# A fused attention and feed-forward block on one core: the second batch's q is biased and squared ahead of the turning of x, and some scaling and transfers change engines

## The chip, the cores and the metric

The kernel runs on one core of a Trainium2 chip. A core has five engines with a queue of instructions each, worked off in order: TensorE (PE in the profile; PEld is its loading of weights), VectorE (DVE), ScalarE (ACT), GpSimd (POOL) and SyncE (SP). In this kernel SyncE and ScalarE also issue the transfers (DMA). The engines wait for one another by semaphores only. The metric is the time of one execution on the device, in microseconds.

## The reference

All arrays are float32. `x` has 8 batches of 1024 tokens of 256 channels.

```python
xn  = layernorm(x)                       # over the 256 channels, eps 1e-5
q, k, v = split(xn @ qkv_w + qkv_b)      # 16 heads of 16
q, k = q / |q|, k / |k|                  # per token and head
kv  = einsum('bhnd,bhne->bhde', k, v)    # no softmax: a 16 x 16 matrix per head
att = einsum('bhnd,bhde->bhne', q, kv) reshaped to (8, 1024, 256) @ proj_w + proj_b
ffn = relu(xn @ W1 + b1) @ W2 + b2       # 256 -> 1024 -> 256
out = x + att + ffn
```

## The kernel before

**Stages and rounds.** The program is one stream of work over the batches, written out by hand in the order in which each engine is to do it; no planner reorders it. For batch b there are two large stages. `hidden(b)` makes relu(xn W1 + b1) (`first_hidden` for batch 0), and `second(b)` multiplies it by W2 and adds the attention, the residual and the bias. Between them stands the projection of the next batch, `project_by_sums(b + 1)`, to q and k. So TensorE's order is: hidden(b), projection of b+1, second(b), hidden(b+1), and so on. Below, *round b* is the time from the first matmul of `second(b)` to the first of `second(b + 1)`.

**Fewer matmuls, more additions.** The products are formed with schemes that need fewer block products (7 for 8, and in `hidden` 26 for 32), at the price of sums of blocks before and after. GpSimd forms most sums of operands: `make_forms` (L319) those of the turned x, named s1A, dA, X1 to X10 and so on; `g_sums` (L693) those for the product of x and k; `sums_of_a` (L239 to L244) those of the hidden values and q. VectorE forms the sums of results out of the banks of PSUM, in `hidden` at L1004, in `second` at L1134 and L1151, and in the product of x and k at L734 (`u_g`, `gT`). In `hidden` several sums read a bank in the midst of its accumulation, so the next product into it waits for that sum; a new product also waits for a free bank among seven.

**From x to the turned x.** For batch b+2, `stats_of` computes mean and variance of the 1024 tokens on VectorE (L344 to L359; the square root on ScalarE, L349). `norm_apply` (L368 on ScalarE, L372 on VectorE) scales the 8 tiles of 128 tokens in place. `turn_x` then transposes 32 by 32 blocks on VectorE (L386, four instructions, one for each fourth j) and moves the blocks between partitions with four transfers for each j, 16 in all (L394), into `xnT`. `shift` (L656, ScalarE) afterwards adds one to half of x's channels in place, which folds a bias into the product of x and k.

**From q to the turned q.** In `second(b)` for batch b+1: `bias_in_bank` (L605) copies a difference of biases into PSUM, `bias_of_q` (L599) adds it to two of four parts of q on VectorE. `norms_of_q` squares the four parts on ScalarE (L504), sums over each head on VectorE (L505), takes maximum, root and reciprocal (`invert`, L465 to L467), and scales q on GpSimd (L624). In `hidden(b + 1)` q is turned as x is (`turn_q`, L386 and L394), at steps set by a table.

**second(b)** runs the products `a`, `c_`, `f`, `d`, the product of x and k (`mix_g_by_sums`: gpa, gpe, gpc, gpd, then gpa and gpd again, L728) and `e`; gpe has its last part between the two halves of `e`. `join` and `turn_back` add a result to `u`, transpose it on VectorE (`yt`, L1142) and add it to the residual on GpSimd (`xq`, L1147); `store` (L1110, SyncE) writes a half of the batch out. The hooks `early`, `mid`, `behind`, `late` and `later` place the work for the following batches; they differ for b of 0, 1 and above:

- b = 0: statistics of batch 2 in `early`, scaling of it in `mid`, `turn_next` (turning of x of batch 2) in `late` with the bias of q of batch 1 behind it; `norms_of_q(1)` in `later`.
- b = 1: bias and norms of q of batch 2 in `early`; statistics of batch 3 and its eight scalings on ScalarE in `mid`; `turn_next` in `behind`.
- b > 1: bias, norms and turning in `early`; statistics of x of batch b+3 in `later`; its scaling after `hidden` of the following round.

**Weights.** In `hidden`, the 26 combinations of W1 lie in DRAM (`w1f`) and are fetched two products at a time into five slots, by `load_w1` (L898) on SyncE. In SyncE's queue in round 0 stand in order: the transfers of the turned x, the load of x of batch 3 (L149), the store of one half, the weights 5 and 6, the store of the other half (which waits for GpSimd's last `xq`), the weights 7, 8 and 9, and the transfers of the turned q.

In `turn_next`, transfer r of each j goes to queue r modulo the number of queues given; before, batch 2 uses SyncE and ScalarE by turns, later batches SyncE alone.

Of the kernel before, what the change touches and what calls it, by code (L numbers as in the profile page):

```python
# [9 lines left out]
F32 = mybir.dt.float32  # L10
# [51 lines left out]
def kernel(  # L62
# [34 lines left out]
    nc = tc.nc  # L97
    P = 128
    B, N, C = x.shape
    H, D = 16, 16  # L100
    assert H * D == C
    INTER = w1.shape[1]
    NT = N // P
    HT = NT // 2
# [13 lines left out]
    one = ctx.enter_context(tc.tile_pool(name="one", bufs=1))  # L118
    work = ctx.enter_context(tc.tile_pool(name="work", bufs=2))
    small = ctx.enter_context(tc.tile_pool(name="small", bufs=2))  # L120
# [15 lines left out]
    def bank(shape, name):  # L136

        return psum.tile(shape, F32, tag="bank", name=name)
# [107 lines left out]
    HM, FH, HC = INTER // 2, FC // 2, C // 2  # L246
# [80 lines left out]
    def more_sums_of_x(b, part):  # L327

        names = [f"X{i}" for i in range(3 + 4 * part, 7 + 4 * part)]
        make_forms(forms_of(b) | more_forms_of(b), names)  # L330
# [29 lines left out]
            for t in tiles:  # L360
                stats[b, t] += (nmr,)

    def norm_apply(b, tiles):
        for t in tiles:
            xt, xn = xs[b][:, t, :], xns[b][:, t, :]
            i, mv, rstd, *nmr = stats.pop((b, t))
            if nmr:
                nc.scalar.activation(  # L368
                    xn, xt, AF.Identity, bias=nmr[0][:, i : i + 1], scale=rstd[:, i : i + 1]
                )  # L370
            else:
                nc.vector.tensor_scalar(  # L372
                    xn, xt, mv[:, i, 0:1], rstd[:, i : i + 1], ALU.subtract, ALU.mult
                )

    class Turn:
# [21 lines left out]
        def step(self, queues=(nc.sync,)):  # L398
            self.square()
            self.move(queues)  # L400
# [3 lines left out]
    def turn_x(b, queues=(nc.sync,)):  # L404

        if b not in xnTs:
            xnTs[b] = big.tile([P, KC, NP, P, 2], F32, tag="xnT", name=f"xnT_{b}")
            turns["x", b] = Turn(xnTs[b], xns[b], f"x_{b}")
        turns["x", b].step(queues)
# [53 lines left out]
    def invert(ss):  # L463

        nc.vector.tensor_scalar_max(ss, ss, L2_EPS * L2_EPS)  # L465
        nc.scalar.activation(ss, ss, AF.Sqrt)
        nc.vector.reciprocal(ss, ss)  # L467
# [30 lines left out]

        return qks[b][:, m, 2 * u : 2 * u + 2, :]

    def squares_of(b, u, m, ss, tag="yt"):
        pool = work if tag == "yt" else one
        sq = pool.tile([P, 2, C], F32, tag=tag, name=f"sq_{b}_{u}_{m}")
        nc.scalar.activation(sq, part_of_qk(b, u, m), AF.Square)  # L504
        return lambda: nc.vector.tensor_reduce(  # L505
            ss[:, 2 * u : 2 * u + 2, :],
            sq.rearrange("p w (g d) -> p w g d", d=D), AX.X, ALU.add,
        )
# [82 lines left out]
            norms_of[b, h, 1] = ss[:, ts(h, HT), :]  # L591
            scale(nc.gpsimd, b, h, 1)

    def bias_of_q(b, bias=None):
        if bias is None:
            bias = bias_in_bank(b)
        for u in (3, 0):
            q1 = part_of_qk(b, u, 0)
            nc.vector.tensor_tensor(  # L599
                q1, q1, bias.unsqueeze(1).to_broadcast([P, 2, C]), ALU.add  # L600
            )

    def bias_in_bank(b):
        bias = bank([P, C], f"dbias_{b}")
        nc.scalar.copy(bias, dbias)  # L605
        return bias

    def norms_of_q(b):
        ss = small.tile([P, NT, H], F32, tag="ssq", name=f"ssq_{b}", bufs=1)
        late = []  # L610
        for u in range(NP):
            late.append(squares_of(b, u, 0, ss, ("u1", "y")[u % 2] if b == 1 else "yt"))
            if len(late) == 2:
                late.pop(0)()
        late.pop(0)()
        invert(ss)
        for h in range(2):
            norms_of[b, h, 0] = ss[:, ts(h, HT), :]
            scale(nc.gpsimd, b, h, 0)
# [492 lines left out]
    def second(b, early=None, mid=None, behind=None, late=None, later=None):  # L1112
# [36 lines left out]
        def join(n, m, bank_, u):  # L1149
            y = tmp("y")  # L1150
            nc.vector.scalar_tensor_tensor(y, bank_, ob[:, 2, m : m + 1], u, ALU.add, ALU.add)  # L1151
            turn_back(n, m, y)
# [112 lines left out]
        u1 = tmp("u1")  # L1265
# [21 lines left out]
        product(e, t1, s1, True, False)  # L1287
        join(1, 1, e, u3)
        next(of_g)
        more_sums_of_x(b + 1, 1)  # L1290
        later()
        store(b, 1)
        product(e, b22, s4, False, True)
        join(0, 1, e, u2)


    warm = bank([P, HT, P], "warm")
# [82 lines left out]
    for b in range(B):  # L1380
# [26 lines left out]
        else:  # L1407
# [3 lines left out]
                norm_apply(b + 2, range(NT))  # L1411
            project_by_sums(b + 1)

        def turn_next():
            if b + 2 < B:
                for _ in range(R):
                    turn_x(b + 2, (nc.sync, nc.scalar) if b == 0 else (nc.sync,))
                shift(b + 2)

        def early():  # L1420
# [14 lines left out]
        def mid():  # L1435
            if b == 0:
                norm_apply(2, range(NT))
                next(of_w1)
                load_first_w1()
            elif b == 1:  # L1440
                stats_of(3)
                norm_apply(3, range(NT))

        def behind():
            if b == 1:
# [1 line left out]

        def late():
            if b == 0:
                bias = bias_in_bank(1)  # L1450
                turn_next()
                bias_of_q(1, bias)
            if b + 3 < B:
                load(b + 3)

        def later():
            if b == 0:
                norms_of_q(1)
            else:
                stats_of(b + 3)  # L1460

# [32 lines left out]
```

## Time and profile before

| | us |
|---|---|
| median of 3 runs (604.47 to 604.97) | 604.96 |
| the profiled execution, its own time | 604.75 |
| its span, first to last instruction | 603.0 |
| round 0 (67.18 to 141.79) | 74.61 |
| round 1 (141.79 to 216.36) | 74.57 |
| round 2 (216.36 to 289.22) | 72.86 |
| round 3 (289.22 to 362.09) | 72.87 |

The profile is one execution. Its instructions are listed by engine, with start and duration counted from the first instruction, the line of the kernel, the operation, the tiles written and read, their shapes, and in brackets the idle time of the engine before the instruction and what ended it. Equal neighbours are merged, with their number behind an x. Matmuls are pipelined and a row's start and end are modelled, so a hole in TensorE's work is best read by laying rows of one round against those of another. `PEclk` is the clock that TensorE was granted, as a share of full speed. In a table by stretches, each engine has its busy time and the number of its instructions; at the end stand the granted clock, the mean busy share of the 16 DMA engines, and GB/s.

### The profile page before, as it was taken

What the parts mean: (1) busy time and instruction counts of PE and PEld (TensorE: products, weight loads), DVE (VectorE), ACT (ScalarE), POOL (GpSimd) and SP (SyncE); (2) the same over time, 40 slices, a digit from 0 to 9 for tenths busy, and PEclk for the clock granted to TensorE, in tenths of its full rate; (3) what the DMA queues carried; (4) which work ended last, traced back from release to release, by engine and by line L of the source; (5) the groups of instructions that cost most, each with busy time, mean ns of one, the idle gap of its engine ahead of it and who ended that gap; (6) DMA issues with size and microseconds to landing.
All of it is one profiled execution on the core that took longest, in us unless ns stands there. A gap on an engine that the chain in (4) does not pass through costs nothing.

```text
span 603.0 us, 7997 instructions
## 1 busy us (share of the span) xinstructions
PE 596.5 (99%) x2385; PEld 413.2 (69%) x2385; DVE 435.4 (72%) x803; ACT 247.4 (41%) x525; POOL 481.0 (80%) x453
## 2 busy tenths in 40 slices
PE   9999999999999999999999999999999999999997
PEld 5466656786568865688566894678846787468746
DVE  7987976878758785577856878388873669537773
ACT  4654332473405851158311673126730373203810
POOL 2859999988976889769897698976989679983470
PEclk9999999999999999999999999999999999999999
DMA  8545367784056733377134780356702667006704
GB/s 289 87 101 140 82 211 206 183 210 55 10 158 170 194 48 70 108 202 179 19 71 139 197 172 6 99 137 178 158 22 49 144 144 148 2 0 164 185 11 95
DMA packets 164810, 73.02 MB, mean 121 GB/s; under 512 B 147488, under 2 KB 152736, under 8 KB 163872
## 3 DMA queue, kind: packets, MB, share of 16 engines
q1 hardware_dynamic: 154432, 67.31, 46.6%
q10 hardware_dynamic: 10336, 5.21, 3.1%
q8 instruction: 19, 0.31, 0.2%
q14 instruction: 23, 0.19, 0.1%
HBM read 44.44 MB, written 11.80 MB: 93 GB/s over the span
## 4 chain that ended last, share of the span: by engine, by line
PE 86%; DVE 6%; POOL 3%; DMA 2%; ACT 1%; issue 1%; ACTq 0%; DVEq 0%; POOLq 0%
PE ph L985 23%; PE poe L1103 9%; PE poa L1103 9%; PE pod L1103 5%; PE poc L1103 5%; PE pof L1103 4%; PE pqe L530 3%; PE pqa L530 3%; PE pqd L530 3%; PE gpd L728 2%; PE gpe L728 2%; PE gpa L728 2%; PE pqc L530 2%; POOL qk L624 2%; PE tok L1213 2%; PE pq L428 1%
## 5 line engine op out<-in xcount | busy, mean ns | idle before, releaser
L1012 ACT ACTIVATE hT<-hT,b_sb 128x256 f32<-128x256 f32 x224 | 95.7, 497 | 56.1 <-DVE hT L1004 56.1
L1004 DVE TENSOR_TENSOR hT<-ph,hT 128x512 f32<-128x512 f32 x84 | 56.0, 687 | 25.1 <-ACT hT L999 21.6
L1004 DVE TENSOR_TENSOR hT<-hT,ph 128x512 f32<-128x512 f32 x77 | 51.8, 679 | 11.1 <-PE ph L985 7.0
L1103 PE MATMUL poa<-hT,w_sb 128*128 128x512 f32 x120 | 56.2, 593 | 0.0
L504 ACT ACTIVATE sq<-qk 128x512 f32<-128x512 f32 x56 | 34.2, 627 | 49.9 <-DVE qk L536 39.8
L1147 POOL TENSOR_TENSOR xq<-xq,yt_o 128x512 f32<-128x512 f32 x29 | 36.5, 1272 | 22.1 <-DVE yt_o L1142 22.1
L985 PE MATMUL ph<-xnT,w_sb 128*128 128x256 f32 x224 | 52.9, 379 | 0.0
L985 PE MATMUL ph<-qk,w_sb 128*128 128x256 f32 x196 | 48.1, 379 | 0.3 <-DMA w_sb<-w1f 0.3
L239 POOL TENSOR_TENSOR hS<-hT 128x512 f32<-128x512 f32 x30 | 38.3, 1276 | 11.5 <-DVE hT L1004 11.5
L985 PEld LDWEIGHTS ph<-xnT,w_sb 128*128 128x128 f32 x224 | 41.9, 190 | 5.5
L985 PEld LDWEIGHTS ph<-qk,w_sb 128*128 128x128 f32 x196 | 37.2, 190 | 5.7 <-POOL Mt L234 0.7
L999 ACT COPY hT<-ph 128x512 f32<-128x512 f32 x49 | 28.1, 574 | 30.4 <-PE ph L985 30.3
L240 POOL TENSOR_TENSOR hS<-hS,hT 128x512 f32<-128x512 f32 x30 | 38.3, 1277 | 2.4
L1103 PEld LDWEIGHTS poa<-hT,w_sb 128*128 128x128 f32 x120 | 22.7, 190 | 25.4 <-issue 22.7
L242 POOL TENSOR_TENSOR hT<-hT 128x512 f32<-128x512 f32 x30 | 38.5, 1310 | 0.0
L1142 DVE STREAM_TRANSPOSE yt_o<-y_o 128x512 f32<-128x512 f32 x29 | 32.2, 1112 | 8.3 <-ACT y_o L1272 6.1
L244 POOL TENSOR_TENSOR hS<-hT,hS 128x512 f32<-128x512 f32 x30 | 37.7, 1290 | 0.0
L985 PE MATMUL ph<-xS,w_sb 128*128 128x256 f32 x140 | 35.1, 381 | 0.2
L624 POOL TENSOR_TENSOR qk<-qk,ssk 128x1024 f32<-128x1024 f32 x14 | 26.8, 1936 | 9.3 <-DVE ssk L467 9.3
L1151 DVE SCALAR_TENSOR_TENSOR y_o<-poe,ob,u_o 128x512 f32<-128x512 f32 x14 | 10.4, 741 | 31.1 <-PE poe L1103 31.1
L1103 PE MATMUL poe<-hS,w_sb 128*128 128x512 f32 x64 | 30.4, 600 | 0.3
L1103 PE MATMUL poc<-hS,w2t 128*128 128x512 f32 x64 | 29.9, 592 | 0.0
(249 smaller groups left out, 1422.4 us busy)
## 6 DMA issues: line engine op xcount, KB each, us to landing
w_sb<-w1f SPq DMA_DIRECT2D x49, 256.0 KB, 3.5
qT<-turn_q SPq DMA_DIRECT2D x128, 64.0 KB, 3.0
x<-in_L_attn_x_dram SPq DMA_DIRECT2D x15, 512.0 KB, 4.6
xq<-in_L_attn_x_dram SPq DMA_DIRECT2D x60, 128.0 KB, 5.0
out_dram<-xq SPq DMA_DIRECT2D x58, 128.0 KB, 2.9
w_sb<-w1f SPq DMA_DIRECT2D x7, 1024.0 KB, 4.9
xnT<-turn_x SPq DMA_DIRECT2D x104, 64.0 KB, 2.1
w1t<-w1f SPq DMA_DIRECT2D x14, 256.0 KB, 5.3
```

Source lines behind the costliest of these rows:

```text
L239: eng.tensor_tensor(s1, a21, a22, ALU.add)
L240: eng.tensor_tensor(s2, s1, a11, ALU.subtract)
L242: eng.tensor_tensor(a21, a11, a21, ALU.subtract)
L244: eng.tensor_tensor(s4, a12, s2, ALU.subtract)
L530: nc.tensor.matmul(dst[:, w, :], f[pairs[g][2][i]][:, :, w], pairs[g][3][i], start=start and w == 0, stop=stop, skip_group_check=True,)
L624: eng.tensor_tensor(part, part, norms_of[b, h, s].unsqueeze(3).to_broadcast([P, HT, H, D]), ALU.mult,)
L728: nc.tensor.matmul(dst, l[:, t, :], r[:, t, :], start=start and t == 0, stop=stop and t == HT - 1, skip_group_check=True,)
L985: nc.tensor.matmul(banks[chain][:, t], w[:, t, :], f[v], start=start and t == 0, stop=n == last[chain], skip_group_check=True,)
L1004: nc.vector.tensor_tensor(block(v), operand(p), operand(q), ALU.add if op == "+" else ALU.subtract)
L1012: nc.scalar.activation(part, part, AF.Relu, bias=b1_sb[:, fc : fc + 1])
L1103: nc.tensor.matmul(dst, l, r, start=start and n == 0, stop=stop and n == len(lhs) - 1, skip_group_check=True,)
L1147: nc.gpsimd.tensor_tensor(xh, xh, yt.rearrange("p u w r c -> p (u w) r c"), ALU.add)
```

## The change

Five edits, all for batches 0 and 1:

1. In `second(0)`, the bias of q of batch 1 and the four squarings come first, and the turning of x of batch 2 after them. The squares no longer use the scratch tiles `u1` and `y`, but four blocks of `hS` (plane 2). The sums over heads, the root and the scaling stay in `later`.
2. In `second(0)`, the last four sums of x of batch 1 (X7 to X10, GpSimd) come at the end, behind the last `join`, and no longer ahead of `later`. On GpSimd they thus stand behind the scaling of q and the last `xq`.
3. In `second(1)`, four of the eight scalings of x of batch 3 are done by VectorE (tiles 0 to 3, L372's form), and ScalarE does tiles 4 to 7 first. On VectorE the four stand between `nmr` and the `yt` of the first result.
4. Of the 16 transfers of the turned x of batch 2, ScalarE issues 4 where it issued 8; SyncE issues 12.
5. Of the 16 of batch 3, ScalarE issues 4 where it issued none; SyncE issues 12.

The number of instructions on every engine stays the same but for the four scalings and the transfers; TensorE's order is unchanged.

```diff
-    def norm_apply(b, tiles):
+    def norm_apply(b, tiles, on_vector=False):
...
-            if nmr:
+            if nmr and not on_vector:
...
-    def squares_of(b, u, m, ss, tag="yt"):
-        pool = work if tag == "yt" else one
-        sq = pool.tile([P, 2, C], F32, tag=tag, name=f"sq_{b}_{u}_{m}")
+    def squares_of(b, u, m, ss, sq=None):
+        if sq is None:
+            sq = work.tile([P, 2, C], F32, tag="yt", name=f"sq_{b}_{u}_{m}")
...
+    def norms_of_second_q():
+
+        ss = small.tile([P, NT, H], F32, tag="ssq", name="ssq_1", bufs=1)
+        late = [
+            squares_of(
+                1, u, 0, ss,
+                hSs[0][:, 2, i].rearrange("p u c w -> p (u c w)").rearrange("p (w c) -> p w c", w=2),
+            )
+            for u, i in enumerate((0, 2, 3, FH))
+        ]
+        yield
+        for step in late:
+            step()
+        invert_and_scale_q(1, ss)
+        yield
+
+    def invert_and_scale_q(b, ss):
         invert(ss)
         for h in range(2):
             norms_of[b, h, 0] = ss[:, ts(h, HT), :]
...
         next(of_g)
-        more_sums_of_x(b + 1, 1)
+        if b > 0:
+            more_sums_of_x(b + 1, 1)
         later()
         store(b, 1)
         product(e, b22, s4, False, True)
         join(0, 1, e, u2)
+        if b == 0:
+            more_sums_of_x(b + 1, 1)
...
+        of_q = []
+
         def turn_next():
             if b + 2 < B:
                 for _ in range(R):
-                    turn_x(b + 2, (nc.sync, nc.scalar) if b == 0 else (nc.sync,))
+                    turn_x(b + 2, (nc.sync,) * 3 + (nc.scalar if b < 2 else nc.sync,))
                 shift(b + 2)
...
             elif b == 1:
                 stats_of(3)
-                norm_apply(3, range(NT))
+                norm_apply(3, range(HT, NT))
+                norm_apply(3, range(HT), True)
...
         def late():
             if b == 0:
-                bias = bias_in_bank(1)
+                bias_of_q(1)
+                of_q.append(norms_of_second_q())
+                next(of_q[0])
                 turn_next()
-                bias_of_q(1, bias)
...
         def later():
             if b == 0:
-                norms_of_q(1)
+                next(of_q[0])
```

## The prediction

> **What bounds the kernel now.** I read the page's busy times first, then the table by rounds, the matmuls in order of time where a round is long, and VectorE, GpSimd and SyncE at those places.
>
> ```profile
> PE 596.5 (99%) x2385; PEld 413.2 (69%) x2385; DVE 435.4 (72%) x803; ACT 247.4 (41%) x525; POOL 481.0 (80%) x453
> ```
> TensorE is the bound, so only its holes can be won. A round is taken from the first `poa` of one batch to that of the next:
> ```profile
> 67.18:141.79 74.61, 73.79 (x300) 51.62 (x299) 59.50 (x117) 33.88 (x75) 70.86 (x65) 1.00 0.73 181
> 141.79:216.36 74.57, 73.56 (x300) 51.94 (x299) 56.22 (x114) 35.04 (x76) 62.07 (x59) 1.00 0.49 117
> 216.36:289.22 72.86, 72.81 (x299) 52.03 (x298) 52.62 (x97) 30.95 (x67) 61.74 (x59) 1.00 0.50 120
> 289.22:362.09 72.87, 72.82 (x299) 52.03 (x298) 52.60 (x97) 30.96 (x67) 61.70 (x59) 1.00 0.49 120
> ```
> The first number is the length. Rounds 0 and 1, which alone the change touches, are 1.75 and 1.71 us over round 2: 3.4 us (0.57%) is all there is to win. TensorE's rows laid against round 2 show where:
> ```profile
> 111.57 1.03 PE L985 MATMUL ph<-xnT,w1t 128*128 128x256 f32 x4
> 112.98 1.10 PE L985 MATMUL ph<-xnT,w1t 128*128 128x256 f32 x4 [0.38 <-DVE hT L1004]
> ...
> 119.25 1.97 PE L985 MATMUL ph<-qk,w_sb 128*128 128x256 f32 x8 [0.30 <-DMA w_sb<-w1f]
> ...
> 168.47 1.13 PE L728 MATMUL gpd<-gt,x 128*128 128x128 f32 x8 [0.60 <-DVE u_g L734]
> ...
> 188.29 1.10 PE L985 MATMUL ph<-xnT,w1t 128*128 128x256 f32 x4 [0.27 <-DVE hT L1004]
> ```
> Round 0 loses 0.54 at 112.98, 0.53 more by 117.82, 0.65 at 119.25: 1.72. Round 1 loses 0.85 at 168.47 and 0.86 from 188.29 to 191.32. VectorE, then GpSimd, around them:
> ```profile
> 106.05 0.95 DVE L467 RECIPROCAL ssq<-ssq 128x128 f32<-128x128 f32 x1 [0.38 <-ACT ssq L466]
> ...
> 110.95 1.31 DVE L386 STREAM_TRANSPOSE turn_q<-qk 128x512 f32<-128x512 f32 x2 [0.59 <-POOL qk L624]
> ...
> 158.13 0.44 DVE L359 SCALAR_TENSOR_TENSOR nmr<-mv,rstd 128x8 f32<-128x8 f32 x1
> 158.50 1.12 DVE L1142 STREAM_TRANSPOSE yt_o<-y_o 128x512 f32<-128x512 f32 x1
> 162.68 2.49 DVE L386 STREAM_TRANSPOSE turn_x<-x 128x512 f32<-128x512 f32 x4 [3.07 <-ACT x L368]
> ...
> 177.68 1.41 DVE L344 BATCH_NORM_STATS2 st<-x 128x6 f32<-128x256 f32 x4 [1.61 <-DMA x<-in_L_attn_x_dram]
> ```
> ```profile
> 107.08 3.83 POOL L624 TENSOR_TENSOR qk<-qk,ssq 128x1024 f32<-128x1024 f32 x2 [0.81 <-DVE ssq L467]
> ...
> 158.50 4.98 POOL L244 TENSOR_TENSOR hS<-hT,hS 128x512 f32<-128x512 f32 x4
> ```
> The reader sees two chains. In round 0 the norms of q come late, GpSimd's scaling of q ends at 110.9, and VectorE's queue stands behind `turn_q`. In round 1 VectorE waits 3.07 us for ScalarE's eight scalings and passes the delay on to `u_g`; later it waits for the load of x, queued on SyncE behind 16 transfers.
>
> **Part 1, round 0: bias and squares lead, last sums later, 12 transfers on SyncE.** On VectorE the two biases (1.25) and four turnings (2.48) change places; both end at 98.1 as before. ScalarE squares from 95.7, when the second bias is done: 4 at 0.63, to 98.1 (before: from 102.10). Their scratch in `hS` was last read by `gpe` and `gpc`, over at 91.5. ScalarE then issues 4 transfers instead of 8 (eight took 5.85, so 2.9) and reaches `shift` at 101.0, as before. VectorE's four reductions start at 100.6, behind `gT`, instead of 102.75, and need 2.5 unhindered. The maximum (0.23) waits for GpSimd to end `xq` (103.4), root 0.31, reciprocal 0.95: 104.8 against 107.0. GpSimd, relieved of X7 to X10 (2.9), scales from 104.9 to 108.7, against 110.9. `turn_q` then never waits, and the add that frees TensorE at 112.98 runs near 111, before it is wanted at 112.43.
>
> What is pushed back: X7 to X10 run at 110.0 to 112.9; the first is wanted at 121.9. GpSimd's sums of x follow 0.7 later and meet two VectorE adds with two SBUF inputs (one such row took 1.08 instead of 0.64 at 114.89); I charge 0.1. SyncE issues 12 transfers, not 8, at 0.66: to 104.4, not 100.6. Behind them the load of x, one store and two loads of weights end at 109.9 instead of 107.75; landing 3.4 later, at 112.1 and 113.3, they precede their matmuls (114.2, 115.9). The turned x lands by 109 (4.5, the slowest but one) and is first read at 114.70; the x loaded 3 us later is read at 154.29. The second store waits for GpSimd's `xq`, now done at 110.0 instead of 112.15; so the third weights are issued at 112.7, not 114.89, and with the 4.22 that they took land at 116.9, before 117.6. Gain: 1.72 - 0.1 = 1.6.
>
> **Part 2, round 1: VectorE scales 4 tiles; 4 of 16 transfers on ScalarE.** ScalarE ends four scalings at 160.6 instead of 162.65 (0.49 apart). VectorE's four stand between `nmr` (158.57) and `yt`, while GpSimd runs without a gap. What one costs depends on that:
> ```profile
> L372 DVE TENSOR_SCALAR x<-x,mv,rstd x7: 404/413/1476, 6.3 to 11.8; 128x256 f32<-128x256 f32 x7
> ```
> ```profile
> 11.85 1.27 POOL L234 TENSOR_TENSOR w1t<-w_sb 128x512 f32<-128x512 f32 x1 [10.55 <-DMA w_sb<-in_L_ffn_W_dram]
> 13.20 1.28 POOL L234 TENSOR_TENSOR w1t<-w_sb,w1t 128x512 f32<-128x512 f32 x1
> ```
> The one of 1476 ns is the only one under a GpSimd add: it began at 11.79 and ended at 13.27, 0.15 after that add. Six without one took 0.41 (0.33 apart). A run of them under a busy GpSimd is not shown; the nearest, two-input adds of both engines in the last stage, go strictly by turns:
> ```profile
> 572.57 1.64 DVE L240 TENSOR_TENSOR hS<-hS,hT 128x512 f32<-128x512 f32 x1
> 574.13 1.75 DVE L239 TENSOR_TENSOR hS<-hT 128x512 f32<-128x512 f32 x1
> 575.92 1.64 DVE L240 TENSOR_TENSOR hS<-hS,hT 128x512 f32<-128x512 f32 x1
> ```
> Bounds: four times 0.33, so 160.0; or each behind one GpSimd add (1.13 to 1.28, and 0.15 for itself): 159.94, then 1.32 each, 163.9. I take the upper end, from the row of the same line.
>
> `yt` (1.12), which filled VectorE's idle time, now comes after, so `turn_x` starts at 164.9 instead of 162.68. From there to the `gpd` matmul took 5.79 (turning, `u3`, `y`, `yt`, two `u_g`): 170.7 instead of 168.47, where 167.70 would be no stall. So 2.2 more is lost. ScalarE, with four transfers (0.73 each, one per turning), `shift` 1.15 and a copy 0.25, is done near 169.5, TensorE's `gpa` (0.89) then ends at 170.4: just covered.
>
> SyncE's 12 transfers run from 165.7 to 173.6, so the load of x goes at 173.7, against 174.09, while the matmuls are 2.2 later; VectorE reaches it at 178.3 and the halves land 3.6 and 4.6 after issue (177.2, 178.8), in time. So the 0.86 from 188.29 on goes. Round 1: +2.23 - 0.86 = +1.37.
>
> **Sum.** -1.6 + 1.37 = -0.2, on the profiled execution's 604.75 (span 603.0 and 1.75 around it; 0.21 under the median 604.96): 604.5.
>
> A rule against the row: the Trainium skill, "SBUF — State Buffer", on the shared port pair, says that whichever of a two-port VectorE operation and a GpSimd one starts first holds the pair for the whole instruction. By it the first scaling (start about 158.49 by the overlap of rows) would go ahead of GpSimd's add (158.50), leaving three waits and the sum of rival B; the row of 11.79 started 0.06 ahead and still waited, so the sum goes by the row. A second: "TensorE: Matmul & The Clock Gate" (Why this matters for your kernels) warns of TensorE gaps over about 3 us, after which the clock halves. The page's clock row is 9 throughout, with no hole over 0.6; half clock for its 3.4 us window would, as an estimate from that page, add 1.7, and make 606.2.
>
> **Rivals.** A is the case above. B: the first scaling slips in behind `nmr` (a small TENSOR_SCALAR at 35.51 did so: 181 ns with a GpSimd add starting): done at 162.8, `gpd` at 169.5, round 1 +0.2, total 603.3. C: no lock in this stage: `turn_x` at 161.1, no stall, both holes gone: -1.6 - 1.7, 601.4; the 1476 speaks against. S, slower: SyncE becomes the bound of round 0. If the third weights are issued after 113.4 (117.6 less 4.22), TensorE waits for them; if they are no sooner than the 114.89 of before, its matmul still starts at 119.25, the 1.6 is not won, and 604.75 + 1.37 = 606.1. The four transfers more on SyncE speak for it, the earlier `xq` against. That the change does nothing is excluded: the orders on four engines differ.
>
> **How the numbers follow.** A 0.42 (604.0 to 605.2), B 0.22, C 0.10, S or another new wait 0.23, something faster that I don't see 0.03. About 0.2% (1.2 us) is what a measurement of this kernel can tell from no change. B, C and the last are faster: 0.35; A is the same: 0.42; S is slower: 0.23. 601.4 to 606.5 leaves out the worst of S and the best of C.
>
> **What will show it.** Round 0 at 72.9 to 73.1 with the scaling of q ending near 108.7 and no wait for `w_sb`; otherwise part 1 is wrong. Everything of round 1 then stands 1.6 earlier: four scalings of x on VectorE of about 1.3 us between 157 and 162.3, `turn_x` at 163.3, `gpd` waiting for `u_g` some 3 us, and round 1 at 75.9. Rows of 0.4 and a round of 72.9 mean C; three long ones and 74.8 mean B; a wait for `w_sb` in round 0 means S. The forecast is most wrong if VectorE is not held four times.

## The result and the profile after

The changed kernel takes 608.40 us (median of 6, 608.02 to 610.65) against 604.97 (604.36 to 605.26) for the kernel before on the same chip: ratio 1.0067, 95% interval 1.0051 to 1.0084. It is slower by two thirds of a per cent; 604.5 was forecast. Timed again on another chip (e9_again below) it took 607.27 (605.80 to 611.05) against 605.23: 1.0043 (1.0025 to 1.0060). The profiled execution took 608.02 with a span of 606.2, against 604.75 and 603.0.

The table of the changed kernel by rounds (stretch, its length, then busy time and number of instructions of TensorE, its weight loads, VectorE, ScalarE and GpSimd; the granted clock; the DMA engines' share; GB/s):

```profile
67.50:141.78 74.28, 73.58 (x299) 51.78 (x298) 59.95 (x117) 33.77 (x75) 70.40 (x65) 1.00 0.71 182
141.78:219.55 77.77, 74.72 (x299) 53.47 (x298) 61.60 (x119) 33.17 (x72) 62.09 (x59) 0.98 0.47 112
```

Round 0 is 0.3 us shorter than before (74.59), not 1.6. Round 1 is 3.2 longer (74.57), not 1.37. The next round is 72.87 again, and so are the later ones. The first `poa` also starts 0.32 later (67.52 against 67.20). That start lies between 67.0 and 68.4 in every profile of this study, whatever the kernel, so it can't be put down to the change. 0.32 - 0.31 + 3.21 = 3.2: the profiled executions' 3.27 is accounted for.

TensorE's rows where these rounds have holes, in order of time (start, length, work, in brackets the idle time before it and what ended it):

```profile
111.89 1.89 PE L999 MATMUL ph<-xnT,w1t 128*128 128x256 f32 x8
...
119.02 1.97 PE L999 MATMUL ph<-qk,w_sb 128*128 128x256 f32 x8 [0.63 <-DMA w_sb<-w1f]
...
169.99 1.57 PE L742 MATMUL gpa<-qk,x 128*128 128x128 f32 x8 [3.00 <-ACT u_g L751]
171.35 1.92 PE L742 MATMUL gpd<-gt,x 128*128 128x128 f32 x8
...
191.09 1.89 PE L999 MATMUL ph<-xnT,w1t 128*128 128x256 f32 x8
```

In round 0 the eight matmuls at 111.89 now run through without the wait that stood at 112.98, so the chain over the norms of q did come sooner. But the third weights hold TensorE at 119.02, within 0.3 us of where they held it before (119.25). In round 1 the hole stands ahead of the second `gpa`, 3.00 us long, and the matmuls after it are slow: `gpd` 1.92 instead of 1.13. The hole that was at 188.29 is gone. The granted clock explains the slow rows (columns as in the table by rounds; the clock is the number ahead of the DMA share):

```profile
166.96:169.99 3.03, 0.03 (x1) 0.00 (x1) 2.90 (x5) 1.30 (x2) 3.03 (x3) 1.00 0.75 166
170.58:173.99 3.41, 3.41 (x16) 2.89 (x15) 0.66 (x3) 0.27 (x1) 3.41 (x5) 0.50 0.43 100
174.00:177.00 3.00, 3.00 (x9) 1.33 (x8) 0.00 (x0) 0.00 (x0) 0.10 (x1) 1.00 0.64 189
```

TensorE is idle for 3.0 us; 0.6 us after it has work again, its clock is 0.50 for 3.41 us, and then 1.00 again. The mean granted clock of every timed execution is on record too: one such fall makes it 0.997 instead of 0.999 or 1.000, and by it the clock fell in all six executions of the changed kernel (once for five of them, twice, 0.994, in the slowest).

SyncE's queue in round 0 (start, time from the first issue of a run to the end of its last, what is issued):

```profile
96.72 8.47 SPq L394 DMA_DIRECT2D xnT<-turn_x  x12
105.30 1.02 SPq L149 DMA_DIRECT2D x<-in_L_attn_x_dram  x2
106.41 2.95 SPq L1124 DMA_DIRECT2D out_dram<-xq  x4
109.46 2.19 SPq L912 DMA_DIRECT2D w_sb<-w1f  x2
111.75 3.23 SPq L1124 DMA_DIRECT2D out_dram<-xq  x4
115.07 1.05 SPq L912 DMA_DIRECT2D w_sb<-w1f  x2
```

From 96.7 on SyncE now has no gap over 0.12 us. In the kernel before it waited for GpSimd ahead of the second store. Now GpSimd's `xq` is ready at 110.28, the queue gets to that store only at 111.75, and the third weights go out at 115.07 (before: 114.89).

VectorE, and then GpSimd, in round 1:

```profile
158.73 5.26 DVE L372 TENSOR_SCALAR x<-x,mv,rstd 128x256 f32<-128x256 f32 x4
163.91 1.11 DVE L1156 STREAM_TRANSPOSE yt_o<-y_o 128x512 f32<-128x512 f32 x1
164.94 2.46 DVE L386 STREAM_TRANSPOSE turn_x<-x 128x512 f32<-128x512 f32 x4
```
```profile
158.74 5.09 POOL L244 TENSOR_TENSOR hS<-hT,hS 128x512 f32<-128x512 f32 x4
```

The four scalings take 1.43, 1.36, 1.35 and 1.35 us, one to each of GpSimd's four adds. The turning of x starts at 164.94, as the forecast had it. ScalarE's queue behind that:

```profile
165.69 2.90 ACTq L394 DMA_DIRECT2D xnT<-turn_x  x4
168.64 1.15 ACT L670 ACTIVATE x<-x,ones 128x1024 f32<-128x1024 f32 x1 [7.72 <-DVE u_o L1148]
169.69 0.25 ACT L751 COPY u_g<-gpa 128x128 f32<-128x128 f32 x1
```

Four transfers, `shift`, then the copy that `gpa` waits for: this, and not VectorE's `u_g`, ends the hole.

### The profile page after: what moved, and what is told of

The parts are those of the page before. It is cut to its first block, busy times and chain, and to the rows that moved or that the text cites. A ratio compares the mean times of both kernels' runs of the same rounds, so it can differ in the third digit from the quotient of the medians.

```text
span 606.2 us, 8001 instructions
## 1 busy us (share of the span) xinstructions
PE 597.9 (99%) x2385; PEld 415.0 (68%) x2385; DVE 440.6 (73%) x807; ACT 245.3 (40%) x521; POOL 480.2 (79%) x453
## 4 chain that ended last, share of the span: by engine, by line
PE 71%; DVE 1%; ACT 0%; ACTq 0%; issue 0%
PE ph L999 22%; PE poe L1117 10%; PE poa L1117 8%; PE poc L1117 4%; PE pod L1117 4%; PE pof L1117 4%; PE pqe L530 3%; PE pqa L530 3%; PE pqd L530 2%; PE gpd L742 2%; PE gpa L742 2%; PE gpe L742 2%; PE tok L1227 2%; PE pqc L530 1%; PE kvp L775 1%; PE mp L792 1%
## 5 line engine op out<-in xcount | busy, mean ns | idle before, releaser
L504 ACT ACTIVATE sq<-qk 128x512 f32<-128x512 f32 x52 | 31.8, 627 | 49.8 <-DVE qk L536 39.9
```

## The experiments

All runs keep the computation. Rounds are measured from the first `poa` matmul of a batch to that of the next, in each run's profiled execution. The ratio is to the kernel before, timed beside each run on the same chip (its medians: 605.58 for e1 to e4, 605.01 for e5 to e8, 605.23 for e9 to e12, 604.62 for e13 to e15).

"Clock fell in" counts, of all timed executions of a kernel, those with a mean granted clock of 0.997 or less.

Three theories are tried. L: in round 1 each of VectorE's scalings waits behind a GpSimd add, and that makes the hole ahead of `gpa`; its rival Q puts the hole down to the four transfers on ScalarE. The clock: the hole lets the granted clock fall to one half, and the fall is not something else's doing. S: in round 0 SyncE's longer queue holds back the third weights; its rival is their landing.

| run | edit | round 0 | round 1 | hole ahead of `gpa` | clock fell in | ratio (95%) |
|---|---|---|---|---|---|---|
| before |  | 74.59 | 74.57 | none | 0 of 83 | 1 |
| after | the change | 74.28 | 77.78 | 3.00 | 6 of 6 | 1.0067 (1.0051 to 1.0084) |
| e1_scalar | ScalarE scales all of batch 3 | 75.20 | 73.56 | 0.43 | 0 of 12 | 0.9983 (0.9973 to 0.9993) |
| e2_vector | before, with VectorE's scalings alone | 74.53 | 76.67 | 1.80 | 4 of 6 | 1.0043 (1.0029 to 1.0057) |
| e3_lead | the lead of bias and squares alone | 73.67 | 74.35 | none | 0 of 9 | 0.9976 (0.9967 to 0.9986) |
| e4_filled | 20 transposes in the hole | 75.61 | 75.70 | 0.39 | 0 of 12 | 1.0011 (1.0002 to 1.0019) |
| e5_behind | GpSimd's sums behind the scalings | 74.58 | 72.87 | none | 0 of 8 | 0.9971 (0.9960 to 0.9982) |
| e6_store | store behind the third weights | 75.18 | 75.83 | 2.70 | 7 of 12 | 1.0041 (1.0021 to 1.0061) |
| e7_both | e5 and e6 | 74.17 | 72.86 | none | 0 of 6 | 0.9967 (0.9953 to 0.9980) |
| e8_two | two tiles on VectorE | 73.36 | 73.29 | 0.17 | 0 of 12 | 0.9977 (0.9967 to 0.9987) |
| e9_again | the change once more | 74.14 | 75.64 | 2.51 | 7 of 11 | 1.0043 (1.0025 to 1.0060) |
| e10_fill8 | 8 transposes in the hole | 74.89 | 75.53 | 1.52 | 6 of 12 | 1.0031 (1.0014 to 1.0048) |
| e11_eight | e5, with 8 transfers on ScalarE | 73.07 | 72.87 | none | 0 of 5 | 0.9954 (0.9939 to 0.9968) |
| e12_load | e11, load of x later | 73.21 | 72.87 | none | 0 of 5 | 0.9956 (0.9940 to 0.9972) |
| e13_five | five tiles on VectorE | 73.23 | 78.83 | 4.05 | 4 of 4 | 1.0083 (1.0062 to 1.0103) |
| e14_six | six tiles on VectorE | 74.71 | 82.05 | 7.38 | 4 of 4 | 1.0109 (1.0092 to 1.0126) |
| e15_third | the change, one more look | 73.21 | 77.53 | 2.74 | 1 of 1 | one time: 606.67 |

### What the scalings on VectorE cost: e1, e2, e5, e8

**e1_scalar**, from the changed kernel:

```
             elif b == 1:
                 stats_of(3)
-                norm_apply(3, range(HT, NT))
-                norm_apply(3, range(HT), True)
+                norm_apply(3, range(NT))
```

> The changed kernel with all eight scalings of x of batch 3 back on ScalarE; everything else as changed. Theory L (VectorE's four scalings, each held behind a GpSimd add, cause the loss of round 1): the eight scalings end near 162.9, the turning of x starts near 163 instead of 164.94, ScalarE's transfers and shift end 2 us sooner, the second gpa matmul starts near 168.2 with a hole of about 1.2 us instead of 3.00, the granted clock stays 1.0; round 1 takes about 74.2 instead of 77.77, total about 604.5. Theory Q (the four transfers on ScalarE, ahead of shift and of the copy that gpa waits for, cause it): gpa still waits 2.5 us or more, round 1 stays above 76.5, total 607 or more. Round 0 stays at 74.3 under both.

ScalarE's copy still comes behind four transfers, yet the hole is 0.43 us and round 1 is 73.56, a whole us shorter than before the change. The transfers on ScalarE are not the loss (theory Q falls). SyncE's four transfers less even win what was lost at the later load of x: 0.86 us before the change, 0.7 in e3, which has all 16 transfers on SyncE, and nothing here.

**e2_vector**, from the kernel before:

```
-                norm_apply(3, range(NT))
+                norm_apply(3, range(HT, NT))
+                norm_apply(3, range(HT), True)
```

> The kernel before with only VectorE's four scalings of x of batch 3 added; transfers and round 0 as before. Theory L: four rows of about 1.35 us, turning of x from about 164.6; without the four transfers ScalarE's copy for gpa comes near 168.5, so the hole ahead of gpa is about 1.7 and another of about 0.9 stands ahead of gpd. If the clock falls only for one long hole: round 1 about 76.8, total 607.2. If these holes suffice to halve the clock: round 1 about 78.2, total 608.6. Theory Q (the scalings on VectorE are hidden, only the transfers on ScalarE cost): 605.0.

TensorE's rows of this run:

```profile
169.89 1.16 PE L728 MATMUL gpa<-qk,x 128*128 128x128 f32 x8 [1.80 <-ACT u_g L737]
171.75 1.13 PE L728 MATMUL gpd<-gt,x 128*128 128x128 f32 x8 [0.70 <-DVE u_g L734]
```

Two holes, 1.80 and 0.70, about as expected, both at full clock in this execution; round 1 is 2.1 longer than before. In four of the run's six executions, though, the mean granted clock is 0.997, so the clock did fall there. This one edit makes the kernel slower (1.0043).

**e5_behind**, from the changed kernel (`last_sums` holds the four sums of h and that of q; `norms_of_q` now ends ahead of GpSimd's two scalings of q and hands them back as a function):

```
-            for i in (1, 2, 0, 3):
-                sums_of_h(b, i, "3")
-            sums_of_q(b, "3")
+            if b != 1:
+                last_sums()
...
-            norms_of_q(b + 1)
+            scales = norms_of_q(b + 1)
+            if b == 1:
+                of_q.append(scales)
+            else:
+                scales()
...
             if b == 1:
+                last_sums()
+                of_q.pop()()
                 turn_next()
```

> The changed kernel with GpSimd's last sums of h (four adds into hS, one into the sums of q) and its two scalings of q of round 1 issued behind the first add of yt to xq, so that GpSimd has nothing to run while VectorE scales its four tiles of x; nothing else changes. Theory L (each scaling waits only because a GpSimd add holds what both need): the four rows fall from 1.35 us to 0.41, the turning of x starts near 161.2 instead of 164.94, no long hole ahead of gpa, clock 1.0, round 1 72.9 to 73.3, total 603.7. If the scalings take 1.35 us for another reason (their source, their scalars), the rows stay and round 1 stays above 77. If GpSimd's sums, now later, are wanted sooner than I think, a new wait of the last poe or gpd matmul stands there and round 1 is 74 or more. Round 0 as in the changed kernel, 74.3 to 75.6.

VectorE in this run, then GpSimd:

```profile
158.33 1.37 DVE L372 TENSOR_SCALAR x<-x,mv,rstd 128x256 f32<-128x256 f32 x4
...
160.65 2.44 DVE L386 STREAM_TRANSPOSE turn_x<-x 128x512 f32<-128x512 f32 x4
```
```profile
157.12 1.26 POOL L711 TENSOR_TENSOR hS<-x,gs 128x512 f32<-128x512 f32 x1
160.79 1.27 POOL L1165 TENSOR_TENSOR xq<-xq,yt_o 128x512 f32<-128x512 f32 x1 [2.41 <-DVE yt_o L1160]
```

The same four instructions on the same data take 1.37 us together instead of 5.26, because GpSimd has nothing to run beside them. Round 1 is 72.87, the length of an undisturbed round: all that the change was to bring there, and all that it lost, hangs on what GpSimd does in those 5 us. GpSimd's sums end 3 us later and nobody waits for them.

**e8_two**, from the changed kernel: `norm_apply(3, range(2, NT))` and `norm_apply(3, range(2), True)`.

> The changed kernel with two tiles of x of batch 3 on VectorE instead of four, and six on ScalarE. Theory L: two waits of 1.35 us, so VectorE is through at 161.4, yt at 162.5, about when ScalarE's sixth scaling ends (161.9); the turning of x starts at 162.5, 2.4 us sooner than with four; gpa waits about 0.5 us, no fall of the clock, round 1 73.2 to 73.6, total 604.2. If the loss does not go with the number of scalings (the mere change of order on VectorE, or the copy of ScalarE, sets it): round 1 stays above 76.

```profile
157.46 2.71 DVE L372 TENSOR_SCALAR x<-x,mv,rstd 128x256 f32<-128x256 f32 x2
...
161.12 2.46 DVE L386 STREAM_TRANSPOSE turn_x<-x 128x512 f32<-128x512 f32 x4
```

Two scalings, two waits, 2.71 us; they are through about when ScalarE's six are. The loss goes with the number of scalings. With two of them round 1 is 0.27 us shorter than with none (73.29 against 73.56 in e1, one profile each); the totals can't tell the two apart.

### Whether the hole brings the clock down: e4, e10, e13, e14, e9, e15

**e4_filled** and **e10_fill8**, from the changed kernel (20 and 8 transposes):

```
+        if b == 3 - 1:
+            filler = bank([P, HT, P], "filler")
+            for i in range(20):
+                nc.tensor.transpose(filler[:, i % HT, :], ident, ident)
         mm(a, a12, b21, False, True)
```

> The changed kernel with twenty transposes on TensorE (written to a bank that nobody reads) ahead of the second gpa matmul of round 1, in the hole of 3.00 us; they take about 2.2 us. Nothing else changes, so gpa still starts near 170.0. If the hole of 3.00 us is what let the granted clock fall to one half for 3.4 us: the clock stays at 1.0, gpa, gpd and the first poe matmuls run at full speed, round 1 is 1.4 to 1.7 shorter (76.1 to 76.4), total 606.8. If the clock falls for another reason: rows of 1.57 and 1.92 stay, total 608.4 or more.

> The changed kernel with eight transposes on TensorE ahead of the second gpa matmul, about 0.9 us of work, which leaves a hole of about 2.1 us. If it takes a hole of about 3 us to let the clock fall: no fall, round 1 as with twenty transposes (75.7 to 76.2), total 606.2, ratio 1.001 to 1.003. If any hole of 2 us suffices: half clock for 3.4 us, round 1 77 or more, total 608.

With 20 transposes:

```profile
168.54 2.35 PE L762 MATMUL filler<-ident 128*128 128x128 f32 x20
171.27 1.16 PE L742 MATMUL gpa<-qk,x 128*128 128x128 f32 x8 [0.39 <-ACT u_g L751]
172.26 1.06 PE L742 MATMUL gpd<-gt,x 128*128 128x128 f32 x8
```

No fall in the profiled execution of either. From the start of `gpa` to that of the second run of `poe` matmuls it takes 3.61 us here (171.27 to 174.88) and 5.25 in the changed kernel (169.99 to 175.24): the fall costs 1.64 us. The other executions part the two runs. With 20 transposes the mean granted clock is 0.999 or more in all twelve, where 14 of the 18 executions of the changed kernel (after, e9 and e15) have a fall: without the hole there is no fall. With 8 transposes six of twelve executions have one, so the hole that was left, 1.52 us in the profile, was not safe; e10's ratio, 1.0031, can't be told from the 1.0043 of e9 on the same chip. Every kernel in the table whose hole is 0.43 us or less has no fall in any execution.

**e9_again**, **e15_third**: the changed kernel, unaltered. **e13_five**, **e14_six**: `norm_apply(3, range(5, NT))` with `norm_apply(3, range(5), True)`, and the same with 6.

> The changed kernel once more, unaltered, beside the three that follow. If the fall of the clock is part of what the change does: a hole of about 3.0 us ahead of gpa, a granted clock of one half for 3.4 us after it, round 1 near 77.7, ratio 1.005 to 1.008. If the fall stands on an edge (2.70 us without a fall, 3.00 with one): in some executions there is none, the times lie in two groups 1.7 us or more apart, and the profile shows round 1 at 75.8 to 76.2.

> The changed kernel, one more look, for the length of the hole ahead of gpa and the granted clock behind it. If the length decides: no fall below about 2.8 us (round 1 75.6 to 76.0), a fall at 3.0 or more (round 1 77.5 or more).

> The changed kernel with five tiles of x of batch 3 on VectorE instead of four. Theory L: one more wait of 1.35 us behind GpSimd, so the hole ahead of gpa is 3.9 to 4.4 us. If the length of the hole sets the fall of the clock (2.70 without, 3.00 with): one half for 3.4 us, round 1 78.6 to 79.2, total 609 to 610. If the fall has nothing to do with the hole: clock 1.0, round 1 77.0, total 607.5 to 608.5.

> The changed kernel with six tiles of x of batch 3 on VectorE. Theory L: two more waits of 1.35 us, hole 5.2 to 5.7 us. If the length of the hole sets the fall: one half for 3.4 us or longer, round 1 80.0 to 80.6, total 610.5 to 611.5. If not: round 1 78.3, total 609 to 610.

The second `gpa` matmul in e9, e15, e13 and e14, one fence each:

```profile
169.70 1.16 PE L742 MATMUL gpa<-qk,x 128*128 128x128 f32 x8 [2.51 <-ACT u_g L751]
```
```profile
168.63 1.29 PE L742 MATMUL gpa<-qk,x 128*128 128x128 f32 x8 [2.74 <-ACT u_g L751]
169.71 1.91 PE L742 MATMUL gpd<-gt,x 128*128 128x128 f32 x8
```
```profile
170.05 1.56 PE L742 MATMUL gpa<-qk,x 128*128 128x128 f32 x8 [4.05 <-ACT u_g L751]
```
```profile
174.74 2.07 PE L742 MATMUL gpa<-qk,x 128*128 128x128 f32 x8 [7.38 <-ACT u_g L751]
```

In these profiles holes of 1.52, 1.80, 2.51 and 2.70 us came without a fall, holes of 2.74, 3.00, 4.05 and 7.38 with one, and each fall made the stretch from `gpa` to the second `poe` run 5.15 to 5.27 us instead of the 3.61 of e9 and e4. It looks like an edge between 2.70 and 2.74, but length alone doesn't settle it. The changes of the clock stand on a grid. In the changed kernel the trace's record of the clock begins at 6.74; the fall at 170.58 comes 48 steps of 3.413 us later and the rise at 173.99 one step after it. In e13, e14 and e15 the record begins at 6.80, 3.92 and 5.68, and the fall comes 48, 49 and 48 such steps later. So the grid stands at another place against the work in each execution. Laid over the holes, it gives this:

| | e14 | e13 | after | e15 | e2 | e6 | e9 | e10 |
|---|---|---|---|---|---|---|---|---|
| hole ahead of `gpa` | 7.38 | 4.05 | 3.00 | 2.74 | 1.80 | 2.70 | 2.51 | 1.52 |
| TensorE busy in the emptiest step of 3.41 us | 0.00 | 0.59 | 0.59 | 0.89 | 1.82 | 2.01 | 2.09 | 2.29 |
| granted clock in the step after it | 0.50 | 0.50 | 0.50 | 0.50 | 1.00 | 1.00 | 1.00 | 1.00 |

The step of e15 and the two of e6 (columns as in the table by rounds, one fence each):

```profile
166.11:169.52 3.41, 0.89 (x8) 0.89 (x9) 3.14 (x6) 1.30 (x2) 3.41 (x3) 1.00 0.67 150
```
```profile
166.17:169.58 3.41, 2.01 (x18) 1.82 (x17) 3.37 (x6) 0.06 (x1) 3.41 (x2) 1.00 0.44 96
169.58:172.99 3.41, 2.11 (x17) 2.08 (x18) 2.08 (x6) 1.51 (x3) 3.41 (x5) 1.00 0.49 113
```

The hole of 2.74 lies in one step but for 0.2 us; the hole of 2.70 is divided between two. In these eight traces a fall followed a step with 0.89 us of work or less, and none a step with 1.82 or more. That is a reading of traces: no run moved the grid on purpose, and nothing between 0.89 and 1.82 was seen. The falls in unprofiled executions of e2 and e10 are not explained by it, as the holes in them are not known. The fall is part of the change's price, in 14 of 18 executions. e9 was expected to show two groups of times; instead the four without a fall (605.80 to 607.27) and the seven with one (606.25 to 611.05) overlap.

e14 missed its numbers upwards, 82.05 instead of 80.0 to 80.6, for a reason that supports theory L. (Its clock also fell for two steps, 6.83 us, from 171.18 on.) VectorE in this run, then GpSimd:

```profile
159.64 9.14 DVE L372 TENSOR_SCALAR x<-x,mv,rstd 128x256 f32<-128x256 f32 x6
```
```profile
158.43 5.04 POOL L244 TENSOR_TENSOR hS<-hT,hS 128x512 f32<-128x512 f32 x4
163.43 1.32 POOL L244 TENSOR_TENSOR hS<-qT,hS 128x512 f32<-128x512 f32 x1
164.71 3.92 POOL L638 TENSOR_TENSOR qk<-qk,ssq 128x1024 f32<-128x1024 f32 x2
```

The first four scalings took 1.43, 1.35, 1.35 and 1.36 us beside adds of 1.3; the fifth and the sixth met GpSimd's scalings of q, of 1.95 each, and took 2.02 and 2.02. In this run each scaling lasted about as long as the GpSimd instruction beside it.

### What holds TensorE in round 0: e3, e6, e7, e11, e12

**e3_lead**, from the changed kernel: transfers and scalings as before the change.

```
-                    turn_x(b + 2, (nc.sync,) * 3 + (nc.scalar if b < 2 else nc.sync,))
+                    turn_x(b + 2, (nc.sync, nc.scalar) if b == 0 else (nc.sync,))
...
-                norm_apply(3, range(HT, NT))
-                norm_apply(3, range(HT), True)
+                norm_apply(3, range(NT))
```

> The first part alone: bias and squares of q ahead of the turning of x and the last sums of x later in round 0; the transfers stay alternating between SyncE and ScalarE in batch 0 and on SyncE alone in batch 1, and ScalarE does all scalings of batch 3. Theory S (in the changed kernel SyncE's twelve transfers of batch 0 delay the issue of the third weights to 115.07 and eat the gain): with eight transfers SyncE is 2.5 to 3 us ahead, the third weights are issued near 113 and land near 117.3, round 0 takes 72.9 to 73.4 instead of 74.28, round 1 74.6 as before, total about 603.4. If the landing of the weights (a busy memory path) and not the issue holds TensorE: the matmul still waits till 118.5 or later, round 0 is 74.0 or more, total 604.5 or more.

Round 0 is 73.67, and no matmul waits for weights. So the first part of the change, alone, does what it was costed at but for the 0.54 us that now wait for VectorE's add to `hT`: two such adds with both inputs in SBUF took 1.51 and 1.14 us, instead of the 0.69 of its other adds, beside GpSimd's sums of x. I had charged 0.1 for that meeting. The expected issue "near 113" was 114.19: the shift stands ahead of the root on ScalarE, so `xq`, which the second store waits for, came 0.5 later.

**e6_store**, from the changed kernel:

```
-        steps[4] += [lambda: store(b - 1, 0)]
+        if b > 1:
+            steps[4] += [lambda: store(b - 1, 0)]
         steps[5] += squares_at(5) + weights(7)
+        if b == 1:
+            steps[5] += [lambda: store(b - 1, 0)]
```

> The changed kernel with one edit on SyncE's queue in round 0: the store of batch 0's first half stands behind the issue of the third weights instead of ahead of it. Theory S (SyncE's queue, not the landing, holds the matmul at 119.02): the third weights are issued near 111.8 instead of 115.07 and land near 115.5, no wait for w_sb is left, round 0 takes 73.2 to 73.7 (a wait of about half a us for VectorE's add to hT may take its place) instead of 74.3 to 75.6; round 1 as in the changed kernel, total 607.2. If the landing is the limit, the weights land as late as before (118.5 or later) and the total is 608.4.

**e7_both**: this and e5's edit.

> Both edits together: GpSimd's sums of round 1 behind VectorE's scalings, and the store of round 0 behind the third weights. If L and S are independent their gains add: round 0 73.2 to 73.7, round 1 72.9 to 73.3, total 602.3 against 605.0 to 605.6 of the kernel before, ratio 0.995. If one gives back what the other wins: 603.5 or more.

SyncE in e6, and TensorE's rows with a wait:

```profile
110.15 3.16 SPq L912 DMA_DIRECT2D w_sb<-w1f  x3
113.40 3.08 SPq L1127 DMA_DIRECT2D out_dram<-xq  x4
116.58 0.56 SPq L912 DMA_DIRECT2D w_sb<-w1f  x1
```
```profile
120.72 1.99 PE L999 MATMUL ph<-xS,w_sb 128*128 128x256 f32 x8 [0.27 <-DMA w_sb<-w1f]
...
127.34 1.99 PE L999 MATMUL ph<-xnT,w_sb 128*128 128x256 f32 x8 [0.88 <-DMA w_sb<-w1f]
```

The third weights went out early (they landed at 116.53) and their matmul did not wait. But the fourth, behind the store, and later ones now hold TensorE, for 0.27 and 0.88 us; e7 shows the same at 126.68 (0.68). Round 0 is not shorter: the wait moved along the queue. e7's ratio, 0.9967, is e5's 0.9971 within the intervals. The round 1 gain is there and round 0 adds nothing: the expected 602.3 was missed (603.13).

**e11_eight**: e5's edit, and `(nc.sync, nc.scalar) if b == 0 else (nc.sync,) * 3 + (nc.scalar if b < 2 else nc.sync,)` for the queues. **e12_load**: also the load of x of batch 3 taken from `late` to product 15 of the next hidden layer.

> GpSimd's sums of round 1 behind VectorE's scalings, as before, and in batch 0 eight of the sixteen transfers on ScalarE instead of four, so that SyncE is relieved in round 0. Theory S: the third weights are issued about 46.1 us after the first poa matmul, and no matmul waits for w_sb; what is left in round 0 is 0.5 to 0.8 of waiting for VectorE's add to hT; round 0 73.4 to 73.7, round 1 72.9, total 602.3, ratio 0.9955. If the transfers' place doesn't matter: round 0 74.2 or more, ratio 0.997 as with GpSimd's sums moved alone.

> As the run with eight transfers on ScalarE, and the load of x of batch 3 is issued near the end of the next hidden layer instead of ahead of the store and the weights (about 1.1 us of SyncE's queue, and its transfer no longer runs beside theirs). Theory S: the weights come another us sooner, but they hold nothing any more, so round 0 stays at 73.4 to 73.7 and the total within 0.3 of the run with eight; by 72.9 to 73.2 the memory traffic of the load was part of the delay. If the load now comes too late for the statistics of batch 3 in round 1: round 1 74 or more.

SyncE in e11:

```profile
96.98 6.57 SPq L394 DMA_DIRECT2D xnT<-turn_x  x8
...
108.34 1.49 SPq L916 DMA_DIRECT2D w_sb<-w1f  x2
...
114.08 1.21 SPq L916 DMA_DIRECT2D w_sb<-w1f  x2
```

In neither run does a matmul of rounds 0 and 1 wait 0.15 us for anything. Round 0 is 73.07 and 73.21, round 1 72.87; 73.4 to 73.7 had been expected for round 0, but the wait for VectorE's add that e3 showed did not come. e11 takes 602.23 us, ratio 0.9954 (0.9939 to 0.9968): it beats both kernels, the one before by 0.46%, or 3.0 us by the medians. The load of x, moved, changes nothing that can be measured (0.9956).

Over all profiled executions with the changed kernel's round 0 (twelve transfers, store ahead of the third weights), the time from the first `poa` to the issue of the third weights goes with the length of the round, but for e9, where later weights hold TensorE (0.36 us at 126.35):

| | e15 | e9 | e13 | e8 | after | e10 | e14 | e5 | e1 | e4 |
|---|---|---|---|---|---|---|---|---|---|---|
| third weights issued after | 46.37 | 46.41 | 46.50 | 46.99 | 47.56 | 47.79 | 47.79 | 47.99 | 48.53 | 48.81 |
| round 0 | 73.21 | 74.14 | 73.23 | 73.36 | 74.28 | 74.89 | 74.71 | 74.58 | 75.20 | 75.61 |

Nothing that differs between these kernels lies in round 0. SyncE alone runs differently, as e15 and e4 show, one fence each:

```profile
96.69 7.89 SPq L394 DMA_DIRECT2D xnT<-turn_x  x12
...
109.33 1.68 SPq L912 DMA_DIRECT2D w_sb<-w1f  x2
...
113.85 1.53 SPq L912 DMA_DIRECT2D w_sb<-w1f  x2
```
```profile
97.09 9.23 SPq L394 DMA_DIRECT2D xnT<-turn_x  x12
...
110.69 2.45 SPq L916 DMA_DIRECT2D w_sb<-w1f  x2
...
116.70 1.14 SPq L916 DMA_DIRECT2D w_sb<-w1f  x2
```

The same twelve issues took 7.89 us in one and 9.23 in the other, and the first issue of weights between 0.91 and 1.97 us, against 0.56 in the kernel before. The longer time of the twelve is that of a single issue: the seventh or eighth takes 1.18 to 1.92 us in six of the ten executions, and all others 0.58 to 0.62. It isn't the number in a row that does it. Among SyncE's eight in e3 and e11 one takes 1.06 and 1.87 as well, and the sixteen in a row of round 1 in the kernel before take 0.58 to 0.61 each. Eight transfers relieve the queue by sending four issues elsewhere: in e3, e11 and e12 the third weights are issued 46.11, 46.30 and 45.55 after the first `poa`, where twelve at their best come to 46.37.

## Why the prediction was wrong

**Part 1, the chain over VectorE, ScalarE and GpSimd: right.** Against the start of the round, which came 0.32 later, the reciprocal ended when forecast (104.8 forecast; 105.14), the scaling of q too (108.7; 109.05) and `xq` (110.0; 110.28). The wait at 112.98 went. The 0.1 charged for sums that meet VectorE's adds was too little: in e3, where no weights hide it, that wait is 0.54.

**Part 1, SyncE's twelve transfers: the first step that failed.** "The third weights are issued at 112.7": they were issued at 115.07, and even in the best execution at 46.37 after the first `poa`, which is 113.6 on before's scale. Three terms were too small. Twelve issues at 0.66 is right only in the undisturbed case (7.89) and was 8.47 here. The two loads of weights took 2.19 instead of the 1.29 they took before. And the second store took 3.23 instead of 2.62, after 1.47 us in which it was ready and the queue was not. I had taken issue times from the kernel before, where none of these issues was stretched. That is rival S, with the mechanism that the forecast gave it, and a chance of 0.23; its deciding point (113.4 on before's scale, 113.7 on this one's) took 4.22 for the landing, which was 3.40 to 4.45 in these runs. e11 against e5, and e3 against e1, undo the queues alone: with eight transfers no matmul waits for weights, and round 0 is 1.51 and 1.53 shorter (one profile each; with twelve it varied between 73.21 and 75.61). The gain of part 1 was 1.4 us where the queue ran well (73.21) and turned into a loss of 1.0 where it did not (75.61).

**Part 2, four waits behind GpSimd: right, and now shown.** The row of 1476 ns, taken against the row of the cheaper case, was the right one: 5.26 for four, 2.71 for two, 9.14 for six, 1.37 without GpSimd. The Trainium skill, "SBUF — State Buffer" (Who interferes with whom), says that a VectorE operation in a two-port mode and a GpSimd one contend for one shared pair of ports and that the one that doesn't get it waits for the whole instruction; these runs agree with that for this `TENSOR_SCALAR` (1.35 us beside GpSimd's adds of 1.3, 0.34 without). Rival B, in which the first scaling slips in, did not come: it took 1.43.

**Part 2, the sum of 1.37: right only where the clock stays, and so the second step that failed.** e9's round 1 is 75.64, against 75.94 forecast (74.57 + 1.37); the 0.86 of the later load of x did come back. The term that failed is the one left out: the forecast named the half clock, at 1.7 from a page, and kept it out of the sum because no hole of that length was in the trace. But the forecast's own terms made such a hole. TensorE's first `gpd` ends at 167.0 (165.93 and 1.06), and the copy by ScalarE was forecast for 169.5: 2.5 us, which is what e9 measured (2.51, no fall), while the other two profiled executions of the changed kernel had 2.74 and 3.00, each with a fall. "Just covered" was said of `gpa` against VectorE's `u_g`, and not asked of TensorE's idleness. The Trainium skill, "TensorE: Matmul & The Clock Gate" (Why this matters for your kernels), warns of gaps over about 3 us. Here one of 2.74 sufficed in one execution and one of 2.70 did not in another, and the place of the hole counted. The price is 1.64 to 1.66 us by the rows of the changed kernel and e15 against e9's; 1.7 had been estimated from that page.

**The sum of the profiled executions.** Forecast 604.5, measured 608.02: 1.3 of round 0 (74.28 against 72.99), 1.8 of round 1 (77.77 against 75.94, of which 1.6 is the clock), 0.3 of the later start. The forecast had priced both failures, S at 606.1 and the fall at 1.7 more, but each by itself; together its own prices make 607.8.

**What stays open.** What stretches single issues of SyncE is not shown. In the kernel before, in e2 and in e12, which takes the load of x away from ahead of the store and the weights, none of these transfers and none of the first weights is stretched; that is one profile each, and no reason. Nor is it shown what makes the slowest executions of the changed kernel. The slowest (611.05) shows one fall by its mean clock (0.997); the slowest without a fall took 607.27, and 1.6 for a fall makes 608.9 of that, so some 2 us have no name. How empty a step of the clock's grid must be for a fall lies, by these traces, between 0.89 and 1.82 us of work.

## What to carry to other kernels

Before work goes from ScalarE to VectorE, look at what GpSimd runs in those very microseconds: the same four scalings cost 1.37 us or 5.26. With GpSimd's sums in the way the split lost 4.2 us of round 1 (77.78 against e1's 73.56); with the sums moved it won 0.7 (72.87). A queue whose issues are counted at their best duration has no slack left to promise; allow for a stretched one, and check what stands last in it. And when the terms of a sum leave TensorE idle for some 2 us or more, the fall of its clock belongs in the sum with a chance, not in a side remark: the fall may come in some executions and not in others, and one profile doesn't tell; the mean granted clock of every execution does.

## What the runs showed of the hardware that was not expected

- In the profiles the clock fell behind holes of 2.74 us and more and not behind 2.70 and less, but it changed only at steps of 3.413 us, and only behind a step with 0.89 us or less of TensorE's work. So the fall came 0.6 us after TensorE had work again in the changed kernel, 0.9 after in e15, and before it had any in e14, where it lasted two steps.
- Kernels with a hole of 1.52 or 1.80 us in their profile had a fall in six of twelve and in four of six executions; 20 transposes in the hole kept the clock up in all twelve.
- Six scalings in a row on VectorE each lasted as long as GpSimd's instruction beside them: 1.35 us beside 1.3, 2.02 beside 1.95. VectorE did not once get two through during one of GpSimd's.
- The same twelve DMA issues of one queue took from 7.89 to 9.23 us in kernels whose code up to there is the same, the difference being one issue of up to 1.92 us among issues of 0.6.
